# A two-layer mixer, attention and gated-FFN kernel on one core: how the first half of the first layer's W2 is put through its Hadamard transform

## The chip, the cores and the metric

The kernel runs on one core of a Trainium2 chip. The metric is the device time of one execution in microseconds; the median of three runs is given. Times inside an execution come from one profiled run and count from the start of its span.

## What is computed

The input x has 4 batches of 512 tokens and 256 features, all in float32. Two layers follow each other. Each normalizes x, computes a branch s and a gate g from it, and adds their product to x:

```python
xn = _layernorm(x, axis=-1)
s = _L0_attn_ref(xn, W_in, W_out, A_theta, B_real, B_imag, C_real, C_imag, norm_w)
g = _silu(_L0_ffn_ref(xn, L0_ffn_W1, L0_ffn_W2, L0_ffn_W3))
x = x + s * g
xn = _layernorm(x, axis=-1)
s = _L1_attn_ref(xn, qkv, o_proj, gamma, beta)
g = _silu(_L1_ffn_ref(xn, L1_ffn_W1, L1_ffn_W2, L1_ffn_W3))
x = x + s * g
```

The branch of the first layer is a mixer that, with its zero start state, comes down to one linear map and an RMS norm; that of the second is causal attention. Both FFNs have the same form, with 1024 hidden features and a Walsh-Hadamard transform (fwht, scaled by 1/sqrt(1024)) between the gate and the last product:

```python
hidden = jax.nn.silu(x @ W1.T) * (x @ W3.T)
out = fwht(hidden) @ W2.T
```

The transform is linear and symmetric, so the kernel transforms W2 once in place of the hidden features of every token.

## The kernel before

**Number format.** TensorE multiplies float32[...] in a rounded form (fp32r). To keep the precision, the kernel splits each operand into a high part, rounded to fp32r by a copy on ScalarE (ACT), and a low part, the remainder, by a subtraction on VectorE (DVE). That is `split` (L59-62); all splits share these two lines. A product of two such pairs is three fp32r products that add up in one PSUM bank (`mm3`, L80-87). All matmuls are recorded at L70 in `in_line`, so groups are told apart by their tiles.

**The transformed W2.** `prep_w2` (L139-171) makes it for one layer, in two halves of 128 output columns. W2 lies in SBUF as 128 partitions by 8 blocks by 128 columns. The transform over the 8 blocks is three butterfly steps on VectorE, each one addition and one subtraction of 512 elements a partition (L151-152, tiles w2b). The transform over the 128 partitions is a product with a 128 x 128 Hadamard matrix on TensorE, in two quarters q of 512 columns (tiles w2ps). The result is split into w2h and w2l (L170), which all the down products of the FFN use. The Hadamard matrix exists twice: `had_f` in float32, loaded at L931, and `had`, its fp32r copy (L962); its entries are exact in fp32r. Three of the four halves (second half of layer 0, both halves of layer 1) split the butterfly's result first, into w2bh and w2bl (L158-160), and multiply each by `had`, both into the same bank. The first half of layer 0 is multiplied natively in float32: `had_f` by the butterfly's result, without a split (L165-166).

**Stages.** Layer 0 runs batch by batch (loop L993-1034), each batch through `ffn` (L461-554): 8 chunks of 128 hidden features, each with 12 products to the two gate banks (tiles f_0gu for the first batch), a silu on ACT (L522), a product on VectorE called the gate here (L523), a split, and 12 down products (tiles f_0dn). Layer 1 (`ffn_s`) has its TensorE order written out by hand. The change lies in the first batch of layer 0. There, weights W1 and W3 are split on the way, one pair of chunks at a time (`split_w13`, L118-130), all down products come after the gates (defer=8), and the low parts of the first four chunks are subtracted late (L539, tiles early).

**What sets the order.** The work beside the FFN is a list of generators whose steps `Beside` (L872-899) shares out over 16 slots, two in each chunk, in proportion to their number:

```python
while self.done < self.total * (k + 1) / self.slots and self.step():
    pass
```

In the first batch the list is `prep_first` (L953-977; 12 steps after its first, which runs ahead), the mixer of batch 0 (3 steps) and the norm of batch 1 (3 steps, among them the bn_stats at L271 and the transposes). `prep_first` runs the steps of `prep_w2` and puts others between them: the cast of `had`, the load of the next x, and `prep_m`, which makes the mixer's matrix (tiles wg, wi, mps). The steps are: three butterflies, two quarters of the first half; three butterflies and the split of the second half; the first part of `prep_m`; a quarter; the rest of `prep_m` (mps); the last quarter.

The order written here isn't the order of issue. When the kernel is built, a scheduler (L1179) plays the instructions through a model of time, takes for each engine what is ready and stands first, and fixes each engine's queue; on the chip each queue runs in that order. `after(ins)` (L458) queues what its block writes on the engine of `ins` behind `ins`. In the first batch the slots of a chunk are behind that chunk's gate on VectorE and behind its last f_0gu product on TensorE (L542, L546), and the weight split of a pair of chunks is behind the gate two chunks before (L497).

**Buffers.** Tiles from `t4` (L44) share ten buffers of 4 KB a partition: raw weights, w2bh and w2bl, wg, wi and others. The butterflies of layer 0 use the four buffers of x (`x_slot`, L92), so that the next batches' x can be loaded only when they are done (L100). Products beside the FFN use three PSUM banks (L56), f_0gu three more and, for chunk 1, the two of f_0dn.

Of the kernel before, what the change touches and what calls it, by code (L numbers as in the profile page):

```python
# [15 lines left out]
F32R = mybir.dt.float32r  # L16
# [5 lines left out]
P = 128  # L22
# [4 lines left out]
NH = H // P  # L27
# [8 lines left out]
def kernel(ctx: ExitStack, tc: tile.TileContext, a: dict, out: bass.AP):  # L36
# [7 lines left out]
    def t4(name, shape, dt=F32):  # L44
        return act.tile(shape, dt, tag="t4", name=name, bufs=10)
# [10 lines left out]
    def psum(name, shape, tag="ms", bufs=3):  # L56
        return ps.tile(shape, F32, tag=tag, name=name, bufs=bufs)

    def split(src, hi, lo, engine=nc.vector):  # L59

        h = nc.scalar.copy(hi, src)  # L61
        return h, engine.tensor_tensor(lo, src, hi.bitcast(F32), ALU.subtract)  # L62
# [5 lines left out]
    def in_line(call, *args, **kwargs):  # L68
        with tc.issue_after(line["last"].ins) if line["fixed"] and line["last"] else nullcontext():
            ins = call(*args, **kwargs)  # L70
        line["last"] = ins
        return ins

    def matmul(*args, **kwargs):
        return in_line(nc.tensor.matmul, *args, **kwargs)
# [19 lines left out]
    def load_x(b, nt=NT, queues=(nc.sync,)):  # L95
        xs[b] = x_slot(f"x{b}", [P, NT, D])
        src = a["x"][b].rearrange("(t p) d -> p t d", p=P)
        for t in range(0, NT, nt):
            queue = queues[t // nt % len(queues)]
            queue.dma_start(xs[b][:, t : t + nt, :], src[:, t : t + nt, :])  # L100

    ident, had_f, mask = (wp.tile([P, P], F32, name=n) for n in ("ident", "had_f", "mask"))
# [5 lines left out]
    had = wp.tile([P, P], F32R, name="had")  # L108
# [23 lines left out]
    def load_w2(layer):  # L132
        raws = []
        for half in range(2):
            raws.append(t4(f"w2raw_{layer}_{half}", [P, NH, P]))
            nc.sync.dma_start(raws[-1], a[f"w2_{layer}"][half])
        return raws

    def prep_w2(layer, raws, dst, scratch):  # L139

        w2h, w2l = dst
        for half in range(2):
            ds_ = slice(half * P, (half + 1) * P)
            cur = raws[half]
            for st, h in enumerate((1, 2, 4)):
                nxt = scratch(f"w2b{st}_{layer}_{half}", [P, NH, P])
                cv = cur.rearrange("p (g two h) d -> p g two (h d)", two=2, h=h)
                nv = nxt.rearrange("p (g two h) d -> p g two (h d)", two=2, h=h)  # L150
                nc.vector.tensor_tensor(nv[:, :, 0], cv[:, :, 0], cv[:, :, 1], ALU.add)  # L151
                nc.vector.tensor_tensor(nv[:, :, 1], cv[:, :, 0], cv[:, :, 1], ALU.subtract)
                cur = nxt
                yield

            native = layer == 0 and half == 0
            if not native:
                bh = t4(f"w2bh_{layer}_{half}", [P, NH, P], F32R)  # L158
                bl = t4(f"w2bl_{layer}_{half}", [P, NH, P], F32R)
                split(cur, bh, bl)  # L160
                yield
            for q in range(2):
                o = psum(f"w2ps_{layer}_{half}_{q}", [P, NH // 2, P])
                qs = slice(q * NH // 2, (q + 1) * NH // 2)
                if native:  # L165
                    matmul(o, had_f, cur[:, qs, :], start=True, stop=True)
                else:
                    matmul(o, had, bh[:, qs, :], start=True, stop=False)
                    matmul(o, had, bl[:, qs, :], start=False, stop=True)
                split(o, w2h[:, qs, ds_], w2l[:, qs, ds_])  # L170
                yield

    def w2_tile(name):
        return wp.tile([P, NH, D], F32R, tag="w2", name=name, bufs=4)

    def w2_tiles(layer):
        return w2_tile(f"w2h_{layer}"), w2_tile(f"w2l_{layer}")
# [9 lines left out]
    def prep_m(win, wout):  # L187

        cb = wp.tile([P, 4, 2, DS], F32, name="cb")
        nc.vector.tensor_tensor(cb, bc[:, :, 0:2, :], bc[:, :, 2:4, :], ALU.mult)  # L190
        cbd = wp.tile([P, 4, DS], F32, name="cbd")
        nc.vector.tensor_tensor(cbd, cb[:, :, 0, :], cb[:, :, 1, :], ALU.subtract)
        g = wp.tile([P, 4], F32, name="g")
        nc.vector.tensor_reduce(g, cbd, AX.X, ALU.add)
        wg = [t4(f"wg{i}", [P, 4, D], F32R) for i in "hl"]
        wi = [t4(f"wi{i}", [P, 4, D], F32R) for i in "hl"]
        for c in range(4):
            nc.scalar.mul(wg[0][:, c, :], wout[:, c, :], g[:, c : c + 1])
            nc.vector.scalar_tensor_tensor(
                wg[1][:, c, :], wout[:, c, :], g[:, c : c + 1], wg[0][:, c, :].bitcast(F32),  # L200
                ALU.mult, ALU.subtract,
            )
        split(win, *wi)
        yield
        hi, lo = (wp.tile([P, 2, D], F32R, name=f"m{i}") for i in "hl")
        o = psum("mps", [P, 2, D])
        for i in range(2):
            mm3(
                o[:, i, :],
                [(tuple(z[:, k, sl(i)] for z in wi), tuple(z[:, k, :] for z in wg)) for k in range(4)],  # L210
            )
        split(o, hi, lo)
        first["m"] = hi, lo
        yield
# [243 lines left out]
    def after(ins):  # L458
        return tc.issue_after(ins.ins) if ins else nullcontext()
# [444 lines left out]
    def call(f, *args):  # L904
        f(*args)
        yield
# [46 lines left out]
    def prep_first():  # L953
        steps = prep_w2(0, raw2, w2, x_slot)
        with after(first["w13"][1]):
            next(steps)
        yield
        for _ in range(4):
            next(steps)
            yield  # L960
        with after(first["silu"]):
            nc.scalar.copy(had, had_f)  # L962
        for _ in range(2):
            next(steps)
            yield
        for _ in range(2):
            next(steps)
            yield
        load_x(1)
        product = prep_m(*raw_m)  # L970
        next(product)
        yield
        next(steps)
        yield
        next(product)
        yield
        yield from steps

    def prep_second():
        qk, vo = load_pair("qk"), load_pair("vo")  # L980
        yield
        qk = split_pair("qk", qk)
        yield
        vo = split_pair("vo", vo)
        yield
        first["wqk"] = product_of_pair("wqk", qk, 1.0 / 16.0)
        yield
        first["wvo"] = product_of_pair("wvo", vo)
        yield
# [3 lines left out]
    for b in range(B):  # L993
        tasks = []
        if b == 0:
            prep = prep_first()
            next(prep)
            tasks.append((prep, 12))
        if b:
            tasks.append((call(gate_all, f"g0_{b - 1}", dn, xns[0, b - 1], xs[b - 1]), 1))  # L1000
        tasks.append((mixer(b), MIXER))
        if b + 1 < B:
            if b:
                load_x(b + 1)
            if b == 2:
                tasks.append((prep_s(0), 4))
            tasks.append((norm(0, b + 1), NORM))
        if b == 0:
            early = w2_tile("early0"), w2_tile("early1")
            spare = [  # L1010
                [early[i][:, 2 * c : 2 * c + 2, :].rearrange("p a d -> p (a d)") for i in range(2)]
                for c in range(NH // 2)
            ]
        if b == 1:
            raw2_1 = load_w2(1)
            w2_1 = w2_tiles(1)
            tasks.append((prep_w2(1, raw2_1, w2_1, t4), W2P))
            tasks.append((prep_second(), 5))
        if b == 2:
            tasks += [(prep_s(1), 4), (norm(1, 0), NORM), (prep_s(2), 4)]  # L1020
        if b == 3:
            atts = [Attention(0)]
            at = atts[0]
            parts = run(at.xt_half, 0), run(at.xt_half, 1), at.xt, at.scaled, at.split_sums
            tasks += [(call(f), 1) for f in parts]
            norms = {1: norm(1, 1)}
            tasks.append((prep_s(3), 4))
        bg = Beside(*tasks)
        if b == 0:
            dn = ffn("f0_0", xTs[0, 0], w13, w2, bg.slot, NH, spare, parts=2, behind=True)  # L1030
        else:
            tail = [run(atts[0].tq, j) for j in range(2)] if b + 1 == B else []
            dn = ffn(f"f0_{b}", xTs[0, b], w13, w2, bg.slot, tail=tail)
        bg.finish()
# [148 lines left out]
```

## Time and profile before

| what | value |
|---|---|
| median of three runs | 361.06 us (361.01 to 361.54) |
| profiled execution: its own time | 361.18 us |
| its span, first to last instruction | 359.4 us |
| granted TensorE clock, mean | 1.00 |
| instructions | 6279 |
| ACT busy | 197.9 us, 55% |
| DMA | 52.25 MB, mean 145 GB/s |
| native products (had_f), as shown | 4 instructions of 592 ns |
| products of w2bh and w2bl with had, as shown | 12 instructions of 394 ns |

In the profile's rows a group has its line, engine, operation and tiles (result first), a count, and a time. Rows of the timeline start with the start and the time from the group's start to its end. PE is TensorE's matmuls, PEld its weight loads, which overlap them. Matmuls are pipelined and their ends are modelled, so distances between starts say more than durations. Rows of the waits give the engine that waited, for whom, the total, the number and the longest. Rows of the windows give, for each engine, busy time and the number of instructions.

### The profile page before, as it was taken

Reading aid. Unit: us, or ns where it says so; the run is one execution under the profiler, and the core shown is the slowest. Engines: PE = TensorE matmul, PEld = TensorE weight load, DVE = VectorE, ACT = ScalarE, POOL = GpSimd, SP = SyncE. Lnnn points to the kernel's source line nnn. Section 1 sums busy time; section 2 is a strip of 40 time slices with the busy share of each in tenths; the row PEclk is TensorE's granted clock in tenths of the full one; section 3 lists DMA queues with packets and bytes.
Section 4 is the critical chain, followed back from the end, with each engine's and each line's share of the span. In section 5 each row is a group of like instructions: output and inputs, shape, how many; then the busy total and the mean of one; then the engine's idle time right before and its main releaser. Section 6 shows DMA issues by size and latency. Waiting matters only on the chain.

```text
span 359.4 us, 6279 instructions
## 1 busy us (share of the span) xinstructions
PE 352.8 (98%) x2477; PEld 327.2 (91%) x2477; DVE 287.5 (80%) x597; ACT 197.9 (55%) x373; POOL 20.8 (6%) x22
## 2 busy tenths in 40 slices
PE   8999999999999999999999999999999999999995
PEld 6878988888988898888999999999999999999995
DVE  6899658998579938998987957989679897568646
ACT  4666156265463425664477655576555676556443
POOL 2000110300020110100100001100011000000000
PEclk9999999999999999999999999999999999999999
DMA  7935000301044317656256136652554645345401
GB/s 237 339 102 192 2 1 2 114 3 60 0 168 172 132 44 249 243 181 191 90 216 253 58 148 207 226 208 95 204 193 162 214 169 204 128 159 196 191 2 58
DMA packets 16285, 52.25 MB, mean 145 GB/s; under 512 B 1633, under 2 KB 7937, under 8 KB 16257
## 3 DMA queue, kind: packets, MB, share of 16 engines
q1 hardware_dynamic: 15968, 51.60, 40.6%
q8 instruction: 19, 0.31, 0.4%
q10 hardware_dynamic: 288, 0.26, 0.2%
q14 instruction: 10, 0.07, 0.1%
HBM read 42.40 MB, written 9.45 MB: 144 GB/s over the span
## 4 chain that ended last, share of the span: by engine, by line
PE 85%; DVE 12%; ACT 1%; DMA 1%; POOL 1%; issue 0%; DVEq 0%
PE f_0gu L70 6%; PE f_1gu L70 6%; PE f_2gu L70 6%; PE f_3gu L70 6%; PE f_3dn L70 6%; PE f_2dn L70 6%; PE f_0dn L70 5%; PE f_1dn L70 5%; PE pv L70 4%; PE o L70 3%; PE tq L70 3%; PE v L70 2%; PE sc L70 2%; PE w2ps L70 1%; PE pt L70 1%; DVE neg L814 1%
## 5 line engine op out<-in xcount | busy, mean ns | idle before, releaser
L70 PE MATMUL f_1gu<-xt,w 128*128 128x512 f32 x96 | 24.9, 396 | 0.3 <-ACT xt L61 0.3
L70 PE MATMUL f_3gu<-xt,w 128*128 128x512 f32 x96 | 25.0, 396 | 0.0
L70 PE MATMUL f_2gu<-xt,w 128*128 128x512 f32 x96 | 24.8, 395 | 0.0
L70 PE MATMUL f_0gu<-xt,w 128*128 128x512 f32 (+1 forms) x108 | 24.3, 378 | 0.0
L70 PEld LDWEIGHTS f_0gu<-xt,w 128*128 128x128 f32 x108 | 18.4, 188 | 4.6 <-issue 1.0
L70 PEld LDWEIGHTS f_1gu<-xt,w 128*128 128x128 f32 x96 | 17.0, 188 | 3.7 <-ACT xt L61 0.5
L70 PEld LDWEIGHTS f_2gu<-xt,w 128*128 128x128 f32 x96 | 17.0, 188 | 3.0
L70 PEld LDWEIGHTS f_3gu<-xt,w 128*128 128x128 f32 x96 | 17.0, 188 | 2.9
L61 ACT CAST f_2hh<-f_2h 128x512 fp32r<-128x512 f32 x16 | 9.9, 622 | 15.6 <-DVE f_2h L523 12.5
L70 PE MATMUL f_3dn<-w2l,f_3hh 128*128 128x256 f32 x64 | 17.7, 281 | 0.0
L70 PE MATMUL f_3dn<-w2h,f_3hh 128*128 128x256 f32 x64 | 17.7, 281 | 0.0
L70 PE MATMUL f_1dn<-w2l,f_1hh 128*128 128x256 f32 x64 | 17.7, 281 | 0.0
L70 PE MATMUL f_2dn<-w2h,f_2hh 128*128 128x256 f32 x64 | 17.7, 282 | 0.0
L70 PE MATMUL f_1dn<-w2h,f_1hh 128*128 128x256 f32 x64 | 17.6, 280 | 0.0
L70 PE MATMUL f_2dn<-w2l,f_2hh 128*128 128x256 f32 x64 | 17.6, 280 | 0.0
L70 PE MATMUL f_3dn<-w2h,f_3hl 128*128 128x256 f32 x64 | 17.0, 281 | 0.0
L70 PE MATMUL f_1dn<-w2h,f_1hl 128*128 128x256 f32 x64 | 17.0, 281 | 0.0
L70 PE MATMUL f_2dn<-w2h,f_2hl 128*128 128x256 f32 x64 | 16.7, 281 | 0.0
L61 ACT CAST f_3hh<-f_3h 128x512 fp32r<-128x512 f32 (+1 forms) x17 | 10.0, 595 | 10.1 <-DVE f_3h L523 6.0
L61 ACT CAST f_1hh<-f_1h 128x512 fp32r<-128x512 f32 x16 | 9.9, 622 | 9.7 <-DVE f_1h L523 6.6
L62 DVE TENSOR_TENSOR f_2hl<-f_2h,f_2hh 128x512 fp32r<-128x512 f32 x16 | 10.9, 680 | 3.9 <-ACT f_2hh L61 3.8
L70 PE MATMUL f_0dn<-w2h,f_0hl 128*128 128x256 f32 x48 | 13.7, 284 | 0.1
(487 smaller groups left out, 1146.1 us busy)
## 6 DMA issues: line engine op xcount, KB each, us to landing
sw<-s SPq DMA_DIRECT2D x32, 896.0 KB, 5.4
s<-sp SPq DMA_DIRECT2D x8, 512.0 KB, 4.0
s<-sp SPq DMA_DIRECT2D x8, 384.0 KB, 2.8
w2raw<-in_w SPq DMA_DIRECT2D x4, 512.0 KB, 5.1
sraw<-in_w SPq DMA_DIRECT2D x4, 512.0 KB, 3.3
mrb<-there SPq DMA_DIRECT2D x4, 512.0 KB, 3.7
w13raw<-in_w SPq DMA_DIRECT2D x3, 512.0 KB, 6.1
x<-in_x SPq DMA_DIRECT2D x3, 512.0 KB, 3.5
```

The lines of the kernel that those rows point to most:

```text
L61: h = nc.scalar.copy(hi, src)
L62: return h, engine.tensor_tensor(lo, src, hi.bitcast(F32), ALU.subtract)
L70: ins = call(*args, **kwargs)
L814: nc.vector.reduce_max(self.neg[:, t : t + 1], self.scs[t][:, : (t + 1) * P], AX.X, negate=True)
```

## The change

The condition `native` and its branch go: the first half of layer 0 is split and multiplied with `had` like the other three. Its `prep_w2` has one step more, so `prep_first` runs three steps rather than four before the cast of `had`, then six rather than four before the next x is loaded, and its share in the list is 13 rather than 12. The tile `had_f` stays, as the source of `had`.

```diff
--- before.py
+++ after.py
@@ -152,21 +152,14 @@
                 nc.vector.tensor_tensor(nv[:, :, 1], cv[:, :, 0], cv[:, :, 1], ALU.subtract)
                 cur = nxt
                 yield
-
-            native = layer == 0 and half == 0
-            if not native:
-                bh = t4(f"w2bh_{layer}_{half}", [P, NH, P], F32R)
-                bl = t4(f"w2bl_{layer}_{half}", [P, NH, P], F32R)
-                split(cur, bh, bl)
-                yield
+            bh, bl = (t4(f"w2b{i}_{layer}_{half}", [P, NH, P], F32R) for i in "hl")
+            split(cur, bh, bl)
+            yield
             for q in range(2):
                 o = psum(f"w2ps_{layer}_{half}_{q}", [P, NH // 2, P])
                 qs = slice(q * NH // 2, (q + 1) * NH // 2)
-                if native:
-                    matmul(o, had_f, cur[:, qs, :], start=True, stop=True)
-                else:
-                    matmul(o, had, bh[:, qs, :], start=True, stop=False)
-                    matmul(o, had, bl[:, qs, :], start=False, stop=True)
+                matmul(o, had, bh[:, qs, :], start=True, stop=False)
+                matmul(o, had, bl[:, qs, :], start=False, stop=True)
                 split(o, w2h[:, qs, ds_], w2l[:, qs, ds_])
                 yield
 
@@ -955,7 +948,7 @@
         with after(first["w13"][1]):
             next(steps)
         yield
-        for _ in range(4):
+        for _ in range(3):
             next(steps)
             yield
         with after(first["silu"]):
@@ -966,6 +959,9 @@
         for _ in range(2):
             next(steps)
             yield
+        for _ in range(2):
+            next(steps)
+            yield
         load_x(1)
         product = prep_m(*raw_m)
         next(product)
@@ -995,7 +991,7 @@
         if b == 0:
             prep = prep_first()
             next(prep)
-            tasks.append((prep, 12))
+            tasks.append((prep, 13))
         if b:
             tasks.append((call(gate_all, f"g0_{b - 1}", dn, xns[0, b - 1], xs[b - 1]), 1))
         tasks.append((mixer(b), MIXER))
```

## The prediction

> **What bounds the kernel now.** I read the busy shares first, then the waits of TensorE, then the stage that the change touches (8 to 50 us), engine by engine. Times are us from the span's start.
>
> ```profile
> PE 352.8 (98%) x2477; PEld 327.2 (91%) x2477; DVE 287.5 (80%) x597; ACT 197.9 (55%) x373; POOL 20.8 (6%) x22
> ...
> PE   8999999999999999999999999999999999999995
> ...
> DVE  6899658998579938998987957989679897568646
> ```
>
> TensorE has work in every slice, VectorE is full only here and there. The waits of TensorE, all of them:
>
> ```profile
> PE warm L70 <- DVE zr L920: 1.5, 1, 1.5
> PE f_1gu L70 <- ACT xt L61: 0.3, 1, 0.3
> PE xt_0tp L70 <- DVE xn L400: 0.3, 1, 0.3
> ```
>
> Two lie before the first product, one near 51. From 7.8 to the tail (some 5 us after 354) the kernel is as long as the matmuls that TensorE is given: an edit that takes matmul time out shortens it by that, and one that loads another engine costs nothing as long as TensorE finds work. How much room the others have, the windows of the stage show (busy PE, PEld, DVE, ACT; instructions in brackets):
>
> ```profile
> 8.00:17.90 9.90, 9.90 (x55) 8.53 (x56) 8.75 (x15) 6.97 (x11) 0.00 (x0) 1.00 0.96 347
> 17.90:21.10 3.20, 3.20 (x12) 1.93 (x11) 3.20 (x5) 1.73 (x4) 0.00 (x0) 1.00 0.03 5
> 21.10:36.00 14.90, 14.90 (x78) 12.56 (x77) 14.90 (x29) 9.81 (x17) 0.00 (x0) 1.00 0.53 177
> 36.00:50.00 14.00, 14.00 (x122) 14.00 (x120) 6.58 (x19) 4.72 (x13) 2.01 (x2) 1.00 0.01 2
> ```
>
> TensorE never stops, but from 17.9 to 36 neither does VectorE. That is the danger of this change: it puts a VectorE instruction into the only stretch where VectorE has no gap. From 36 to 50 VectorE is idle for more than half.
>
> **What the Trainium skill says.** "FP8 and Floating Point Precision", in its part on FP32, gives a true fp32 product four passes through the array. The trace agrees: such a product stands there as two instructions, together 0.86 us against 0.233 for one fp32r product of the same size (3.7 times). "Perfetto Trace Analysis", Tensor Engine Instruction, says that the end shown for a matmul is an estimate; so I price TensorE by the distance of starts, not by the 592 ns in the rows. "VectorE: DVE Perf Modes", perf-mode tier table, has fp32 `tensor_tensor` in the 1x mode; the trace's 1.21 us for 1024 elements is such a rate, so no cheap form of the added subtraction is to be hoped for.
>
> **Part 1, the products of the first half (L163-169).** From TensorE's timeline (start, duration, group):
>
> ```profile
> 17.75 1.02 PE L70 MATMUL w2ps<-w2b,had_f 128*128 128x512 f32 x2
> 18.21 1.97 PE L70 MATMUL f_0gu<-xt,w 128*128 128x512 f32 x6
> 20.02 1.02 PE L70 MATMUL w2ps<-w2b,had_f 128*128 128x512 f32 x2
> 20.47 6.86 PE L70 MATMUL f_0gu<-xt,w 128*128 128x512 f32 x27
> 27.18 0.39 PE L70 MATMUL w2ps<-w2bh,had 128*128 128x512 f32 x1
> 27.41 2.26 PE L70 MATMUL f_0gu<-xt,w 128*128 128x512 f32 x9
> 29.51 0.39 PE L70 MATMUL w2ps<-w2bl,had 128*128 128x512 f32 x1
> ```
>
> Nine f_0gu from 27.41 to 29.51 make 0.233 each. From 17.75 to 20.02 are 2.27; less six f_0gu (1.40) leaves 0.87 for one native product. From 20.02 to 27.18 are 7.16; less 27 f_0gu (6.30) leaves 0.86. The native half costs 1.73. The new form is one fp32r product for each of bh and bl: 27.18 to 27.41, 0.23. Four of them are 0.93. **TensorE gains 0.80.** The weight loads stay four.
>
> **Part 2, the split added (L160).** The other half shows it, on ACT and VectorE:
>
> ```profile
> 24.49 1.05 ACT L61 CAST w2bh<-w2b 128x1024 fp32r<-128x1024 f32 x1 [0.71 <-DVE w2b L152]
> ...
> 26.38 1.21 DVE L62 TENSOR_TENSOR w2bl<-w2b,w2bh 128x1024 fp32r<-128x1024 f32 x1
> 27.51 0.68 DVE L62 TENSOR_TENSOR f_0hl<-f_0h,f_0hh 128x512 fp32r<-128x512 f32 x1
> ```
>
> ACT gets 1.05, VectorE 1.13 by starts (26.38 to 27.51). ACT is idle from about 17.15 (end of a silu that starts at 16.55) to 17.95, just when the third butterfly step is done (17.1): the cast fits there and pushes the next silu back by about 0.25, which delays a PSUM bank that TensorE wants at 19.4 at the earliest, so nothing.
>
> VectorE's 1.13 is the open cost. What it delays, and the cover:
> - The weight splits of L122. That of the fourth pair is pinned behind the gate of chunk 4 (L497, L946), ran 25.11 to 26.33, and chunk 6 of f_0gu starts at 20.02 + 0.86 + 24 x 0.233 = 26.5. Its low part is first used by the fourth matmul of a bank, so two banks give six matmuls (1.40) ahead of it: cover 1.55. Needed, if the split slips by the whole 1.13 while TensorE is 0.80 early: 1.93. A stall of at most 0.4. But the gate is what VectorE is given as soon as TensorE has finished chunk 4, and the added step is queued ahead of it long before; I expect the butterflies of the second half to slip in its place. Their product waits for 27.2 and 29.5, with f_0gu left as other work. Taken: 0; bounds 0 and 0.4.
> - The late subtractions of the first four chunks (L539) and the rest of the tail:
>
> ```profile
> 33.23 1.28 DVE L539 TENSOR_TENSOR early<-f_0h,early 128x512 fp32r<-128x512 f32 x2
> 34.44 1.39 DVE L271 BATCH_NORM_STATS2 ln_1st<-x 128x6 f32<-128x256 f32 x4
> ...
> 37.54 1.28 DVE L539 TENSOR_TENSOR early<-f_0h,early 128x512 fp32r<-128x512 f32 x2
> ```
>
> TensorE starts on the third chunk's down products near 38.7 and needs its low part about 39.1; it is there at 38.2. Cover 0.9, needed 1.93: a stall of 1.0 if all slips. But ahead of it stand four bn_stats of the next batch (1.31 by starts) that nobody waits for before the transposes at 49.5; they can go behind, and the 1.13 vanish there. Taken: 0; bounds 0 and 1.0 (this is the same lag as above, not added to it).
> - VectorE's end of the stage, 40.3, and the batch's xn (41.5 to 42.9) move back by up to 1.13; the transposes come at 49.5, now 48.7. Cover over 4.
>
> **Part 3, the steps moved (L958-968, L998).** The stage shares out 12+3+3 = 18 steps over 16 slots, then 19. By L894 both products of the first half go one slot later (slots 1, 2 to 2, 3), the second half's first two butterflies too (3, 4 to 4, 5); its last butterfly, split and first product stay (5, 6, 8), the product M and the second half's last product go one later (8, 9 to 9, 10), the mixer stays at 10. One consequence on VectorE: the first butterfly of the second half (17.04 to 18.24) falls behind the gate of chunk 2, which can then run at 17.2 instead of 18.24 after 0.1 to 0.2 of idleness. Of the rest, each ran later than its new slot allows already. Cost 0, bounds -0.2 and +0.2 for another interleaving. `had` is cast behind the same silu (14.22), before either product wants it, and its source had landed by then. No DMA is moved past another: load_x(1) still follows the second split. Its issue on SP waits for butterflies (21.29 before); 1.1 later means landing near 26 with 3.5 us of transfer, needed at 34.4. The next two x loads and w2raw of the second layer queue behind it on SP; the latter is needed at 57.5. Two more t4 tiles: ten buffers, eight taken by loads at 17, two free, and four freed before the next ones at 24.5. Cost 0.
>
> **Sum.** -0.80 + 0 + 0 = -0.80. The profiled execution took 361.18 (span 359.4 and 1.8 around it): 360.38. The median of the runs is 0.12 lower, 361.06, so 360.26, said as **360.3**. That the wait of 0.3 at 51 shrinks is possible, not counted.
>
> About 0.2% is what a measurement of this kernel can tell from no change: 0.72 us, so below 360.34 or above 361.78. The forecast lies almost on the first line; half of its own case falls on either side.
>
> **Rivals.**
> - *Half the gain goes into the lag* (0.22). VectorE's 1.13 slips to the places above, TensorE stalls 0.4 at chunk 6 up to 1.0 in the down products: 360.7 to 361.3. For it: VectorE has no gap from 17.9 to 36. Against: the bn_stats stand there as filler.
> - *VectorE becomes the bound of the stage* (0.18), slower. One mechanism: the order laid down when the kernel is built puts the added 1.21 ahead of weight splits and gates, every later gate is late by 1.13, PSUM banks of f_0gu come free late, and TensorE follows VectorE from about 20 to 40. Then the 0.80 is idled away and the delay paid: 361.06 + 1.13 = 362.2. It decides once stalls pass 1.5 (0.80 + 0.72), that is with next to none of the covers of 1.55 and 0.9 left. Against: these covers, and 6.6 of 14 busy on VectorE after 36.
> - *TensorE doesn't gain 0.80* (0.05): if the two short products per bank were paced by their weight loads, they would cost more than 0.23; the second half speaks against it. 361.0.
> - *The full gain or a little more* (0.55): 359.9 to 360.6.
>
> **How the numbers follow.** Likeliest 360.3, its own range 359.9 to 360.6. Eight in ten: from 359.9 through the second case and into the rise of the third, 361.7. Faster by over 0.2%: somewhat over two thirds of the full-gain case (0.40) and a little luck from the new order (0.03): 0.43. Slower: most of the VectorE case, 0.16. The rest, 0.41, within.
>
> **What would show it.** Right: no w2ps matmul of the had_f kind, eight products of each of bh and bl as 0.39 rows, TensorE's busy time down by 0.8, TensorE's waits still three, bn_stats of ln_1 later than 34.4, the last f_0dn matmul starting near 50.1 instead of 50.9. Wrong: a wait of PE f_0gu or f_0dn on DVE (w of L62, early of L539, a gate of L523) between 20 and 40; or f_1gu beginning no earlier than 51.5.

## The result and the profile after

The changed kernel takes **361.77 us** (median of 16 runs, 361.53 to 362.36), the kernel before 361.18 beside it (16 runs, 361.01 to 361.62): ratio 1.0017, 95% interval 1.001 to 1.0023. It is slower by 0.6 us; the forecast was faster by 0.8. The profiled execution took 361.86 us, its span 360.1.

Of the page after, the busy shares:

```profile
PE 353.2 (98%) x2477; PEld 327.4 (91%) x2477; DVE 288.8 (80%) x598; ACT 198.2 (55%) x374; POOL 20.8 (6%) x22
```

This line hides what happened. The products were shortened, and yet TensorE's busy time went up, from 352.8 to 353.2: it is summed over modelled ends. Distances between starts tell more. From the first f_0gu to the first f_1gu, which I call **the stretch**, the kernel before takes 7.83 to 51.49, 43.66 us, the changed one 7.72 to 52.15, 44.43. From there to the end of the span both take 307.9. The whole loss, 0.77 in the profiled pair, lies in the stretch.

TensorE's waits after:

```profile
PE warm L70 <- DVE zr L913: 1.4, 1, 1.4
PE f_1gu L70 <- ACT xt L61: 0.3, 1, 0.3
PE f_0gu L70 <- DVE f_0h L516: 0.3, 1, 0.3
PE mps L70 <- ACT wih L61: 0.2, 1, 0.2
```

Two are new: f_0gu for a gate on VectorE (L516 after, L523 before), and the product M (mps) for wih. The windows of the same stages as before:

```profile
8.00:17.90 9.90, 9.90 (x55) 8.45 (x54) 8.37 (x14) 7.35 (x12) 0.00 (x0) 1.00 0.98 353
17.90:21.10 3.20, 3.20 (x15) 2.57 (x15) 3.20 (x5) 1.57 (x3) 0.00 (x0) 1.00 0.03 7
21.10:36.00 14.90, 14.39 (x69) 11.10 (x68) 14.90 (x26) 9.89 (x18) 0.00 (x0) 1.00 0.51 172
36.00:50.00 14.00, 14.00 (x120) 14.00 (x119) 7.58 (x23) 4.44 (x13) 2.01 (x2) 1.00 0.02 7
```

VectorE has still no gap from 17.9 to 36. It has one a little earlier (8.37 of 9.90, before 8.75). TensorE, which had no gap from 21.1 to 36, now has 0.51. Its timeline shows where (start, duration, group, wait):

```profile
19.81 0.63 PE L70 MATMUL w2ps<-w2bh,had 128*128 128x512 f32 x2
20.27 2.26 PE L70 MATMUL f_0gu<-xt,w 128*128 128x512 f32 x9
22.38 0.63 PE L70 MATMUL w2ps<-w2bl,had 128*128 128x512 f32 x2
22.84 5.77 PE L70 MATMUL f_0gu<-xt,w 128*128 128x512 f32 x24
28.59 0.51 PE L70 MATMUL w2ps<-w2bh,had 128*128 128x512 f32 x1
29.37 1.67 PE L70 MATMUL f_0gu<-xt,w 128*128 128x512 f32 x6 [0.28 <-DVE f_0h L516]
30.88 0.40 PE L70 MATMUL w2ps<-w2bl,had 128*128 128x512 f32 x1
31.50 0.74 PE L70 MATMUL mps<-wgh,wih 128*128 128x256 f32 x4 [0.23 <-ACT wih L61]
```

The four new products take 0.46 for each pair by starts (19.81 to 20.27, 22.38 to 22.84), 0.92 in all against 1.73: the gain of 0.80 is there. But the product at 28.59 is followed after 0.78 where 0.23 would do, the one at 30.88 after 0.62, and small losses of 0.1 to 0.15 surround them (the first, 0.15, before the product at 28.59, which waits for w2bh); up to 34.5 they sum to about 1.5. That is 0.80 and the 0.77 together.

VectorE's rows of the stage, those that matter:

```profile
17.56 0.69 DVE L516 TENSOR_TENSOR f_0h<-f_0h,f_0gu 128x512 f32<-128x512 f32 x1 [0.50 <-ACT f_0h L515]
18.16 0.69 DVE L151 TENSOR_TENSOR w2b<-w2raw 128x512 f32<-128x512 f32 x1
...
20.50 1.22 DVE L62 TENSOR_TENSOR w2bl<-w2b,w2bh 128x1024 fp32r<-128x1024 f32 x1
...
28.51 0.21 DVE L187 TENSOR_REDUCE g<-cbd 128x4 f32<-128x64 f32 x1
28.64 0.68 DVE L516 TENSOR_TENSOR f_0h<-f_0h,f_0gu 128x512 f32<-128x512 f32 x1
```

At 17.06 VectorE goes idle for 0.50, because the first butterfly of the second half, which used to fill this wait for a silu, now stands behind the gate. At 20.50 is the added subtraction. At 28.51 and 28.64 are g, at 26.25 before, and the gate of chunk 5, at 28.11 before. This gate's inputs had been ready since about 25.8 (the silu ends at 25.47, and the last product of chunk 5 starts at 25.41); the instructions queued ahead of it are the second half's last butterfly, w2l twice and a split. The chain of work that ended last, which before was TensorE alone from 8 us to 50, now runs through this queue (start, duration, what):

```profile
27.39 0.60 DVE w2l L62
27.99 0.60 DVE f_0hl L62
28.59 0.14 DVE g L187
...
29.22 1.30 ACT wgh L191 x3
30.52 0.94 ACT wih L61
31.46 0.04 issue
31.50 0.86 PE mps L70 x5
```

Late steps of VectorE stop TensorE in two ways. One is the gate of chunk 5, which frees the bank that chunk 7's first f_0gu products fill at 29.37. The other goes through ACT, which makes wgh and then wih from g. g comes last there, but not by much: ACT had first to make the second half's w2bh, whose butterfly was late as well.

```profile
27.49 1.05 ACT L61 CAST w2bh<-w2b 128x1024 fp32r<-128x1024 f32 x1 [2.02 <-DVE w2b L152]
```

From its end at 28.54 ACT waits another 0.27 for g.

**Theory:** the stage was nearly balanced. VectorE's queue had less than a microsecond to spare against TensorE at the gate of chunk 5, and about two (wih done at 29.20, mps at 31.14) on the way to mps; the shorter products bring TensorE 0.8 nearer to it, the subtraction and the move put the queue back. **Rivals:** the move of the steps alone; ACT's added cast; one misplaced instruction, which another order mends.

### The profile page after: what moved, and what is told of

It reads as the page before. It is cut to its first block, busy times and chain, and to the rows that moved or that the text cites. A ratio compares the mean times of both kernels' runs of the same rounds, so it can differ in the third digit from the quotient of the medians.

```text
span 360.1 us, 6282 instructions
## 1 busy us (share of the span) xinstructions
PE 353.2 (98%) x2477; PEld 327.4 (91%) x2477; DVE 288.8 (80%) x598; ACT 198.2 (55%) x374; POOL 20.8 (6%) x22
## 4 chain that ended last, share of the span: by engine, by line
PE 84%; DVE 13%; ACT 2%; POOL 1%; issue 1%; DVEq 0%; ACTq 0%
PE f_1gu L70 6%; PE f_2gu L70 6%; PE f_3gu L70 6%; PE f_3dn L70 6%; PE f_2dn L70 6%; PE f_0dn L70 5%; PE f_1dn L70 5%; PE f_0gu L70 4%; PE pv L70 4%; PE o L70 3%; PE tq L70 3%; PE v L70 2%; PE sc L70 2%; PE warm L70 1%; PE pt L70 1%; PE w2ps L70 1%
## 5 line engine op out<-in xcount | busy, mean ns | idle before, releaser
L70 PE MATMUL f_2dn<-w2l,f_2hh 128*128 128x256 f32 x64 | 17.6, 281 | 0.0
```

## The experiments

Each ran beside the kernel before, whose median was 361.12 to 361.25; a median is of 4 to 21 executions, of 19 to 41 for the kernel before. "Stretch" is from one profiled execution, 43.66 before and 44.43 after, so it need not be that of the median.

| run | median | ratio and 95% interval | stretch |
|---|---|---|---|
| e1_no_sub | 361.08 | 0.9996 (0.9988 to 1.0004) | 43.71 |
| e2_move_only | 361.36 | 1.0004 (0.9996 to 1.0012) | 43.63 |
| e3_no_move | 363.25 | 1.0061 (1.0049 to 1.0074) | 45.65 |
| e4_dve_only | 362.51 | 1.0034 (1.0021 to 1.0048) | 45.02 |
| e5_act_only | 361.22 | 1.0000 (0.9992 to 1.0009) | 43.65 |
| e6_no_subs | 360.78 | 0.9987 (0.9981 to 0.9994) | 42.90 |
| e7_before_no_sub | 360.88 | 0.9991 (0.9983 to 0.9999) | 43.33 |
| e8_both_native | 361.34 | 1.0005 (0.9996 to 1.0013) | 43.90 |
| e9_g_early | 362.58 | 1.0038 (1.0026 to 1.0051) | 44.32 |
| e10_pool_both | 365.34 | 1.0112 (1.0096 to 1.0127) | 45.96 |
| e11_pool_before | 361.59 | 1.0010 (1.0003 to 1.0017) | 44.55 |
| e12_late_w2l | 362.20 | 1.0028 (1.0017 to 1.0040) | 45.47 |
| e13_pool_first | 362.72 | 1.0041 (1.0029 to 1.0054) | 45.39 |
| e14_no_sub_pin | 363.14 | 1.0056 (1.0043 to 1.0068) | 45.69 |
| e15_before_pin | 363.72 | 1.0074 (1.0062 to 1.0087) | 44.50 |
| e16_after_pin | 363.17 | 1.0056 (1.0043 to 1.0068) | 45.81 |
| e17_no_sub_no_move | 360.54 | 0.9984 (0.9978 to 0.9991) | 43.03 |
| e20_nomove_g | 361.93 | 1.0022 (1.0013 to 1.0030) | 43.63 |

### One part at a time

**e1_no_sub**: the changed kernel without the added subtraction.

```diff
...
-            split(cur, bh, bl)
+            if layer == 0 and half == 0:
+                nc.scalar.copy(bh, cur)
+                bl = bh
+            else:
+                split(cur, bh, bl)
```

> The changed kernel without the added subtraction on VectorE: the first half's bl isn't made, and its second product reads bh again, so this half of W2 is multiplied by twice its rounded form. TensorE and ACT have the same work as in the changed kernel, VectorE 1.13 us less. If VectorE's queue is what cost the changed kernel its gain: the waits on the gate and on wih go, and the 0.80 of TensorE appears, about 360.4 where before is 361.2. If ACT's added cast (1.05) or the moved steps are the cause: about 361.8 as the changed kernel. If the short products don't save 0.80: 361.0 to 361.2 without waits.

It took 361.08, the time of before. The subtraction is most of the loss, but without it the gain of TensorE is still missing. In VectorE's timeline the idle time ahead of the gate of chunk 2 is still there:

```profile
17.80 0.69 DVE L522 TENSOR_TENSOR f_0h<-f_0h,f_0gu 128x512 f32<-128x512 f32 x1 [0.69 <-ACT f_0h L521]
```

**e2_move_only**: the kernel before with an empty step in the first half (an `else: yield` beside the split), and the steps counted as in the change: the move alone.

> The kernel before with an empty step where the split would be, so that the steps move as in the change (13 shares, three steps ahead of the cast of had) and no work is added or taken away. If VectorE's added work is the cause: 361.2, as before. If the move is the cause (the second half's butterflies behind the gate of chunk 2, 0.5 of VectorE idle at 17): 361.7 to 362.6.

No difference, and the stretch is 43.63. Alone, the move costs nothing.

**e4_dve_only** and **e5_act_only**: the kernel before, with an instruction on VectorE or on ACT whose result nobody reads, where the split would be. The diff shows e4's; e5 has `nc.scalar.copy(bx, cur)` instead.

```diff
+            if native:
+                bx = t4("w2bx", [P, NH, P], F32R)
+                nc.vector.tensor_tensor(bx, cur, cur, ALU.subtract)
```

> The kernel before with one added subtraction of 128x1024 on VectorE at the place of the split, into a tile that nobody reads; native product and steps as before. If VectorE's queue is the cause: TensorE is 0.80 less early than in the changed kernel, so of the lost 1.5 about 0.7 remain, 361.9; the gate of chunk 5 and g are again late. If ACT's cast or the move is the cause: 361.2.

> The kernel before with one added cast of 128x1024 on ACT at the place of the split, into a tile that nobody reads. If VectorE's queue is the cause: 361.2. If ACT's 1.05 is the cause (silus late, PSUM banks late, wih late): 361.9.

ACT's cast costs nothing. The subtraction costs 1.26 us, its whole 1.13 by starts and a little more, in a kernel in which TensorE is not early at all. e5 takes the same extra tile from the shared buffers, so the tile is not the cause. By starts, e4 loses 0.26 at the gate of chunk 5, 0.26 at the first products of chunk 5, 0.18 at the weight split of the fourth pair and 0.70 at down products near 32 that wait for w2h and w2l: the loss has no single place.

**e17_no_sub_no_move**: e1 with the cast and the first quarter as one step and 12 shares, so that every step keeps its old place: the short products alone.

> The changed kernel without the added subtraction (the low product of the first half reads bh again) and with the steps where they are in the kernel before (the cast to bh and the first quarter are one step, 12 shares): VectorE's queue is nearly that of the kernel before, TensorE has 0.80 less. If it is VectorE's amount of work that holds TensorE to 43.7: 43.7 again, 361.1. If it was the move, which puts VectorE's first butterfly of the second half behind a gate that comes late: stretch 42.9 to 43.1, 360.5.

360.54, ratio 0.9984, and TensorE's waits are those of before:

```profile
PE warm L70 <- DVE zr L920: 1.5, 1, 1.5
PE f_1gu L70 <- ACT xt L61: 0.3, 1, 0.3
```

So Part 1 of the prediction was right to 0.2: 0.63 of the 0.80 come out in the stretch. From here two steps lead to the result: the move then costs 0.43 (0.9984 to 0.9996), the subtraction 0.76 more (0.9996 to 1.0017).

### How much room there was

**e6_no_subs**: the changed kernel without the subtraction in either half of layer 0 (the copy of e1, for `layer == 0`).

> The changed kernel without the subtraction for bl in either half of layer 0 (the low products read bh again, so this W2 is multiplied by twice its rounded form). TensorE's work as in the changed kernel, VectorE 2.27 us less, 1.13 less than in the kernel before. If TensorE's 0.80 was swallowed because VectorE paces this stage as well: now it has room, the stretch from the first f_0gu to the first f_1gu falls from 43.7 (before) to 42.9 and the time to about 360.4. If the short products don't save 0.80 in this place, or something else than VectorE holds TensorE (PSUM, ACT's casts): 43.5 to 43.7 and 361.1.

With 1.13 of VectorE's work less than before, the move does no harm that can be measured: 360.78, close to e17. The stretch of 42.90 is that of the fastest of its 21 executions (360.35).

**e7_before_no_sub**: the kernel before without the second half's subtraction, by the same copy.

> The kernel before without the subtraction for bl in the second half of layer 0 (its low product reads bh again). TensorE's work as before, VectorE 1.13 less. If TensorE alone bounds the kernel before: 361.2, stretch 43.7. If VectorE bounds it: down by up to 1.1, 360.1.

0.3 us. The stretch shrinks by 0.33, the wait at f_1gu that the profile of before shows and this one does not. So before, VectorE's load was not costing TensorE anything in the middle of the stage, and still e4 shows that 1.13 more of it did: there was little room between the two.

**e8_both_native**: the kernel before with both halves of layer 0 native (`native = layer == 0`, with an empty step in the second half's place).

> The kernel before with the second half of layer 0 multiplied natively as well, the steps unchanged: VectorE 1.13 and ACT 1.05 less, TensorE 0.80 more. If TensorE bounds the stage before: 362.0, stretch 44.5. If VectorE does: 361.2 or less.

This is the change done the other way round: 0.80 of TensorE's work more, 1.13 of VectorE's less, and no difference in the median that can be measured. The stretch is 0.25 longer; against e7, which also has 1.13 less on VectorE, it is 0.57 longer, most of the 0.80.

### One place, or the amount?

**e9_g_early**: the changed kernel with the three small instructions that make g put at the cast of `had`.

> The changed kernel with the three small VectorE instructions that make g put behind the gate of chunk 1, at the cast of had, so that wgh and wih on ACT don't wait for g at 28.5. If the late g made the wait for wih and that wait was worth its 0.5 on the path: stretch 43.9 instead of 44.4, about 361.3. If VectorE's queue as a whole is late by the added 1.13, the wait only moves to another place (the gate of chunk 5, wil, w2bl): within 0.2 of the changed kernel, 361.7.

By starts the wait of mps for wih shrinks from 0.40 to 0.17. It does not go, because ACT still makes the late w2bh first and starts wgh at 28.70, against 28.81 in the changed kernel. The gate of chunk 5 costs 0.42, and a silu near 18 costs 0.47. In the stretch it regains 0.11 of 0.77. The rest of its time was lost far behind the stage; see the last section.

**e12_late_w2l**: the changed kernel with the two w2l subtractions of the first half put off until the second half's last quarter, so that they do not stand ahead of the gate of chunk 5.

> The changed kernel with the two subtractions for w2l of the first half put off behind the gate of chunk 5 (VectorE has the same work in another order). If it is the order that counts, gates behind preparation: the gate of chunk 5 comes 1.2 earlier, TensorE's wait of 0.55 before chunk 7 goes, stretch 43.9. If it is the amount: TensorE waits as much at the next places (w2bl, wih, wil, mps), stretch 44.4 or more.

The wait for the gate is gone. In its place TensorE loses 0.47 ahead of the product of w2bl and 0.37 at 37.9, where the mixer's product waits for mh on ACT; that of mps for wih stays, at 0.32. Its stretch also holds 1.12 lost before 18.5 us, 0.41 of it a wait for a silu, so its size tells little; the places tell more: most of the wait moved along the queue.

**e3_no_move**: the changed kernel with the split and the first quarter as one step and 12 shares: the subtraction without the move, nothing left out.

```diff
             split(cur, bh, bl)
-            yield
+            if layer or half:
+                yield
...
-        for _ in range(3):
+        for _ in range(2):
...
-            tasks.append((prep, 13))
+            tasks.append((prep, 12))
```

> The change with its added split, but with the split and the first quarter of the first half as one step, so that the list has 12 shares and every later step keeps its old place. If the loss is the added 1.13 of VectorE and the move together (the two runs without the added subtraction lie 0.54 apart), taking the move back leaves the short products' -0.6 and the subtraction's +0.8 to +1.3: 361.3 to 361.9, a ratio of 1.000 to 1.002, and VectorE without the idle 0.5 before the gate of chunk 2. If the move was the whole cause, 360.6, ratio 0.9985. If the added subtraction alone was, 361.8 as in the changed kernel, ratio 1.0017.

363.25: none of the three. Without the move the same subtraction costs 2.7 us instead of 0.76. TensorE's timeline and VectorE's:

```profile
34.33 0.28 PE L70 MATMUL mps<-wgl,wih 128*128 128x256 f32 x1
35.97 0.39 PE L70 MATMUL f_0dn<-w2l,early 128*128 128x256 f32 x1 [1.36 <-DVE w2l L62]
```

```profile
29.82 0.21 DVE L188 TENSOR_REDUCE g<-cbd 128x4 f32<-128x64 f32 x1
...
32.35 1.39 DVE L265 BATCH_NORM_STATS2 ln_1st<-x 128x6 f32<-128x256 f32 x4
33.67 1.65 DVE L193 SCALAR_TENSOR_TENSOR wgl<-wout,g,wgh 128x256 fp32r<-128x256 f32 x4
35.24 0.67 DVE L62 TENSOR_TENSOR w2l<-w2ps,w2h 128x512 fp32r<-128x512 f32 x1
```

Here g is made at 29.82, and the order fixed when the kernel is built puts the four bn_stats of the next batch ahead of wgl and w2l. TensorE has work up to w2l and then stands still; by starts it loses 1.52 there, 0.61 at mps waiting for wih, and 0.38 at a down product waiting for w2h. These are the bn_stats that the prediction counted on to go behind.

**e20_nomove_g**: e3 with g early.

```diff
+    g = wp.tile([P, 4], F32, name="g")
+
+    def prep_g():
...
+        prep_g()
```

> The same, and the three small instructions that make g put at the cast of had instead of ahead of the matrix M. In the changed kernel g came 2.3 later than before and TensorE's product mps waited for what follows from it. If the late g is what is left of the loss, this is the version that keeps some of TensorE's 0.8: 360.6 to 361.0, ratio 0.9985 to 0.9995. If the amount of VectorE's work is the cause, the wait shows at another place (the gate of chunk 5 or the low part of the second half) and it is 361.3 to 361.9, ratio 1.000 to 1.002.

In the stretch this is the best of all versions that do the whole split: 43.63, that of the kernel before, and mps no longer waits for wih. TensorE loses 0.31 by starts at the gate of chunk 5, 0.17 at a silu near 17.6, and 0.14 at a late subtraction of the third chunk (early, 39.4). Against e17 the subtraction still costs 0.60 there. The median is no better, 361.93, for the same cause behind the stage as in e9.

### GpSimd in VectorE's place

**e10_pool_both** (the subtraction of both halves of layer 0), **e13_pool_first** (the added one) and, from the kernel before, **e11_pool_before** (the second half's) put it on GpSimd (the diff is that of e13):

```diff
-            split(cur, bh, bl)
+            split(cur, bh, bl, nc.vector if layer or half else nc.gpsimd)
```

> The changed kernel with the subtractions for bl of both halves of layer 0 on GpSimd. Nothing is left out; VectorE has 2.27 us less than in the changed kernel. If VectorE's load is all that swallowed TensorE's 0.80, and GpSimd takes no more than some 3 us for one: as the run without both subtractions, stretch from the first f_0gu to the first f_1gu 42.9, 360.8. If GpSimd is slow enough that the second half's low product comes late, or slows VectorE beside it: 43.7 or more, 361.2 to 362.

> The changed kernel with the added subtraction alone on GpSimd: VectorE's work as in the kernel before, TensorE's 0.80 less. Nothing is left out. If VectorE paces the stage as much as TensorE does before: nothing gained over the kernel before, as in the run without that subtraction, stretch 43.7, 361.1. If only the added 1.13 had swallowed the gain: stretch 42.9, 360.4.

> The kernel before with the second half's subtraction of layer 0 on GpSimd, the first half native. If TensorE bounds the stage before, VectorE's relief is worth only the wait at the start of the next batch, as in the run without that subtraction: stretch 43.3 to 43.7, 360.9 to 361.2. If GpSimd is slow: the low product of the second half late, 361.5 or more.

All three are slower than the kernel before. VectorE is relieved of 1.13 and loses more, since its instruction beside GpSimd's stops. GpSimd's and VectorE's rows of e13_pool_first:

```profile
19.01 2.57 POOL L62 TENSOR_TENSOR w2bl<-w2b,w2bh 128x1024 fp32r<-128x1024 f32 x1 [12.22 <-ACT w2bh L61]
```

```profile
19.24 2.89 DVE L152 TENSOR_TENSOR w2b<-w2raw 128x512 f32<-128x512 f32 x1
22.05 1.21 DVE L62 TENSOR_TENSOR w<-w13raw,w 128x1024 fp32r<-128x1024 f32 x1
```

The butterfly takes 2.89 in place of 0.68, and TensorE waits 1.7 for the weight split behind it. e10 shows the same; in e11 it is the gate of chunk 5 that waits, and TensorE 0.6 for it. e10 loses 1.9 more behind the stretch (309.8 in place of 307.9), at a gate and at low parts of the later batches that VectorE makes too late. So these runs don't show what the change would cost with VectorE relieved.

### An experiment that missed

**e14_no_sub_pin**, **e15_before_pin** and **e16_after_pin** were to take out the idle 0.5 of VectorE at 17. The silu it waits for stands on ACT behind the cast of the third weight pair, which waits for its transfer. So the casts were queued behind the silu of chunk 1, in e1, before and after:

```diff
+            if c == 1:
+                first["silu_1"] = first["silu"]
...
-            with after(first["w13"][0]), after(first["w13"][1]):
+            with after(first["w13"][0]), after(first["w13"][1]), after(first.get("silu_1")):
```

> The changed kernel without the added subtraction (bl of the first half isn't made, its low product reads bh again), and with ACT's casts of the later weight pairs queued behind the silu of chunk 1, so that a late transfer of these weights doesn't hold up that silu, chunk 2's silu and its gate on VectorE. Without the pin this kernel gained 0.17 of TensorE's 0.80. If the late transfer on ACT's queue and the 0.7 of VectorE's idleness that follows it took the rest: stretch 42.9 to 43.1, 360.4 to 360.6. If VectorE's amount of work alone holds it: stretch 43.7, 361.1.

> The kernel before with the same pin on ACT alone. TensorE has no wait there in this kernel, so neither theory gives it more than 0.2: stretch 43.5 to 43.7, 361.0 to 361.2.

> The changed kernel with the pin on ACT alone; nothing is left out. If the late transfer is a good part of the changed kernel's loss of 1.4: stretch 43.7 or less, 361.1 or less. If VectorE's added 1.13 makes it: at best the 0.5 of idleness at 17 is won, stretch 43.9 to 44.4, 361.3 to 361.8.

The pin also caught the second pair, which TensorE needs at once: all three wait 1.1 for it. In e15 another 1.7 is lost behind the stretch, at the same places as in e10. They settle nothing. The late transfer alone is not the cause: ACT waited 1.10 for it in the changed kernel, 1.20 in e2 and 0.99 in e17 (0.53 before), and e2 and e17 lose nothing by it that the stretch shows. What it adds to the cost of the move stays open.

## Why the prediction was wrong

**Part 1 held.** 0.80 by the starts, 0.58 to 0.63 in the time when nothing else changes (e17).

**Part 2 failed: "Taken: 0".** The added subtraction costs 1.26 alone (e4), 0.76 in the change (e1 to after), 2.7 without the move (e17 to e3) and, by stretches, 0.60 in the best order found. In the changed kernel the two covers held: the weight split of the fourth pair ran at 24.24, earlier than before, and the third chunk's down products did not stop. But they were not the nearest limits. I looked for places where the split's own lag would be felt, and counted no cover for the gates, which free TensorE's banks, nor for g. How little room there was can be read from the timelines, as the distance between a start on VectorE and the start on TensorE that needs it: the gate of chunk 5 and chunk 7's first f_0gu, the gate of chunk 4 and chunk 6's first, the weight split of the fourth pair and the first product that reads its low part (the fourth of chunk 6).

| kernel | gate of chunk 5 | first f_0gu of chunk 7 | distance | gate of chunk 4 to chunk 6 | weight split to its product |
|---|---|---|---|---|---|
| before | 28.11 | 29.74 | 1.63 | 1.97 | 2.30 |
| e2, the move alone | 29.09 | 30.05 | 0.96 | 1.30 | 1.63 |
| e17, the short products alone | 28.17 | 29.10 | 0.93 | 1.25 | 1.59 |
| e1, short products and move | 28.88 | 29.61 | 0.73 | 0.74 | 1.28 |
| after | 28.64 | 29.37 | 0.73 | 2.00 | 2.10 |
| e4, the subtraction alone | 29.43 | 30.18 | 0.75 | 0.86 | 1.28 |
| e3, the change without the move | 28.09 | 28.82 | 0.73 | 2.58 | 2.68 |
| e20, e3 with g early | 28.10 | 28.83 | 0.73 | 2.21 | 2.29 |

The rows of the kernel before:

```profile
28.11 0.68 DVE L523 TENSOR_TENSOR f_0h<-f_0h,f_0gu 128x512 f32<-128x512 f32 x1
29.74 1.56 PE L70 MATMUL f_0gu<-xt,w 128*128 128x512 f32 x6
```

No kernel of the table comes below 0.73 at a gate or 1.28 at the split: these are the limits, the instruction's own time and the way to TensorE. So the kernel before had 0.90 to spare at the gate of chunk 5, 1.24 at that of chunk 4 and 1.02 at the split. Each is less than the 1.93 that I needed. At the split I had counted 1.55, since I took six products to stand ahead of its first use; in the order of the kernel before there are three and one of w2bh.

The shorter products take about 0.70 of each room, the move alone 0.67. One of the two fits, both together do not: this is why the move costs nothing in e2 and 0.43 between e17 and e1. Where e1 loses it, its timelines show:

```profile
25.28 0.68 DVE L522 TENSOR_TENSOR f_0h<-f_0h,f_0gu 128x512 f32<-128x512 f32 x1
25.88 1.22 DVE L62 TENSOR_TENSOR w<-w13raw,w 128x1024 fp32r<-128x1024 f32 x1
```

```profile
20.96 6.02 PE L70 MATMUL f_0gu<-xt,w 128*128 128x512 f32 x24
26.82 0.39 PE L70 MATMUL w2ps<-w2bh,had 128*128 128x512 f32 x1
27.16 2.37 PE L70 MATMUL f_0gu<-xt,w 128*128 128x512 f32 x9
29.37 0.40 PE L70 MATMUL w2ps<-w2bl,had 128*128 128x512 f32 x1
29.61 1.67 PE L70 MATMUL f_0gu<-xt,w 128*128 128x512 f32 x6
```

The 24 products take 5.86 by starts, where 24 x 0.233 are 5.59: chunk 6 waits for the gate of chunk 4. From 26.82 to 29.37 another 0.2 goes to the weight split, and about 0.1 behind 29.61 to the gate of chunk 5 (mps starts at 31.12). Together that is some 0.6 of the 0.68 by which the stretches of e17 and e1 differ. The waits of the profile show none of it. In the changed kernel the scheduler queues the gate of chunk 4 early (23.64), and the gate of chunk 5 takes the lag.

The second place is mps. g slipped from 26.25 to 28.51, wih on ACT from 28.16 to 30.42, and mps at 31.50 waited for it. Before, wih had been done 2 us ahead of mps. g is only part of that: with g early, e9 still loses 0.17 there, because w2bh holds ACT; in e20, where the butterflies are earlier too (w2bh at 26.48), the wait is gone. The wait at the gate stays in both.

The filler did not help either. I had said that the four bn_stats can go behind; in the changed kernel they stand where they stood, and the late subtractions behind them slipped from 37.54 to 39.20.

**"I expect the butterflies of the second half to slip in its place"** was half right. They slipped, the last one from 23.18 to 26.11, and with it w2l and a split, to where they stand ahead of that gate; the product of w2bh, for which I saw other work, waited 0.15. Work that slips without harm to its own consumer harms what it is put in front of.

**Part 3 failed: "Cost 0, bounds -0.2 and +0.2".** The step named in it, the first butterfly behind the gate of chunk 2, did happen; the idle time was 0.50 rather than the 0.1 to 0.2 I gave it, and the cost 0.43 when TensorE is early, more than the bound. But it is not a cost by itself: with the subtraction in place, the order without the move is worse by 1.5 (e3 against after). The order is computed anew for each text, so the costs of parts do not add up.

**The rivals.** "VectorE becomes the bound of the stage" is the mechanism that came true, at 361.8 rather than 362.2, and at another place: not weight splits and every gate from 20 on, but one gate near 28 and, through ACT, g and w2bh. What I held against it, "6.6 of 14 busy on VectorE after 36", did not count, since the work that was late was wanted before 32. Of the signs I gave beforehand, the wrong ones appeared: f_0gu waiting on a gate, and f_1gu beginning at 52.15, later than 51.5. Of the signs for right, "TensorE's busy time down by 0.8" was badly chosen: it went up by 0.4. The chances did not agree with each other either: the text has half of the full-gain case on each side of the 0.2% line, and the chance of "faster" takes over two thirds of it.

**What stays open.** Whether an order exists in which the split costs less than TensorE gains. None of the versions tried that do the whole work is faster than the kernel before.

## What to carry to other kernels

An engine with no wait is the bound only as far as the others have room to follow: measure that room, as the distance from a buffer's release to its next use, less the least that this distance can be, at every handover of the stage, and take an expected gain off each of them before adding anything to the queue behind. In this stage, where two engines both had no gap, shifting work from one to the other gained nothing in either direction (the change, and e8). Where a scheduler lays the order, what is added is paid by whatever ends up behind it, so the consumers of all that slips have to be listed, not only those of the added instruction.

## What was not expected of the hardware

**GpSimd stops VectorE.** In three runs a tensor_tensor of GpSimd on 128 x 1024, shown with 2.56 to 2.98 us, held up the VectorE tensor_tensor that began beside it until it was done: 2.89 and 2.88 in place of 0.68 in e13 and e10, 2.77 in e11. In e13 GpSimd ends at 21.58, VectorE's instruction, begun at 19.24, at 22.13. The Trainium skill says so in "SBUF — State Buffer", Who interferes with whom: a VectorE instruction with two SBUF inputs contends with a GpSimd instruction that reads SBUF, and the order of issue decides which of them blocks. These three agree, and GpSimd seems to wait too: in each, its instruction ends 2.26 after the end of the VectorE instruction that was running when it began (19.32 and 21.58 in e13). In e10's second subtraction (29.86, 2.98 us) VectorE's split is shown to start 0.02 later and takes its usual 0.67, so there GpSimd seems to have waited; spans of GpSimd are rough.

**A stop of TensorE costs more than the wait shown.** Before the product at 29.37 the changed kernel's profile shows a wait of 0.28, while the distance of starts is 0.55 too long. And the next distance is too long as well, 0.34 in place of 0.23 (29.37 to 29.71). The 0.1 is the same behind a stop of 1.90 (e13, a wait for a weight split) and behind stops that the list of waits leaves out, as those of e1.

**The same matmuls at another pace.** In e9 and e20 TensorE needs 0.9 us more from the first f_1gu to the end of the span (308.8 in e20, 307.9 before), though it waits for nothing new there. The timelines of e20 and of before in layer 1:

```profile
215.16 0.88 PE L70 MATMUL f_0gu3g<-tb,sw 128*128 128x256 f32 x6
215.88 0.28 PE L70 MATMUL f_0dn<-w2h,f_0hh 128*128 128x256 f32 x1
```

```profile
215.42 0.86 PE L70 MATMUL f_0gu3g<-tb,sw 128*128 128x256 f32 x6
216.12 0.28 PE L70 MATMUL f_0dn<-w2h,f_0hh 128*128 128x256 f32 x1
```

Six products take 0.72 against 0.70 by starts, and so on through layer 1, little by little: after 200 us products of 256 columns follow each other at 119.5 ns in both, at 118.0 before. Both kernels take g's tile of 16 bytes a partition from its pool earlier than the others do, so that what is allocated behind it lies elsewhere; no other kernel here shows the drift. That the addresses are the cause is only a guess; it was not tried.
